# The first image of a two-layer state-space kernel: its convolution split over four engines, and the next image's norm placed ahead of it

## Chip, cores and metric

The kernel runs on one core of one Trainium2 chip (trn2). The metric is the device time of one execution in microseconds (us); less is better. Engines are named as in the profile: PE (TensorE; PEld its weight loads), DVE (VectorE), ACT (ScalarE), POOL (GpSimd), SP (SyncE, which here only issues DMAs).

## What is computed

Eight images of 64 x 64 positions and 96 channels go through two layers. Each layer normalizes the image in groups (32 groups of 3 channels, over the whole image), projects it to 192 channels and a gate z of 192, runs a depthwise 3 x 3 convolution with Silu over the 192, scans the result in four directions with a state of 16 per channel, sums the four, normalizes over channels, multiplies by Silu(z), projects back to 96 and adds the input. Cut to what matters here (layer 0):

```python
def _gn(v, G=32, eps=1e-5):
    g = v.reshape(B_, H_, W_, G, C_ // G)
    m = jnp.mean(g, axis=(1, 2, 4), keepdims=True)
    s = jnp.var(g, axis=(1, 2, 4), keepdims=True)
    return ((g - m) / jnp.sqrt(s + eps)).reshape(v.shape)
...
xz = x @ in_proj_w.T
xp, z = (xz[..., :Di], xz[..., Di:])
xc = conv_general_dilated(xc, conv_w, (1, 1), 'SAME', feature_group_count=Di) + conv_b
xc = _silu(xc)
...
dA = jnp.exp(d_t[..., None] * A)
h = dA * h + d_t[..., None] * B_e * u_t[..., None]
...
x = x + _L0_conv_ref(_gn(x), ...)
```

## The kernel before

Channels lie on partitions: 192 channels are two halves of C = 96 (NH = 2), positions run along the free axis. An image has L = 4096 positions, in four tiles of T = 1024 or eight of MM = 512[...].

The program is `begin`, then for each image the scan (`scan_rows`), and between two images `between`, which finishes one layer and makes the first deltas of the next image; `finish` ends the last image. The convolutions of later images are made piece by piece beside the scan (`conv_beside`, L1001), so only two convolutions stand alone: that of image 0 in `begin` (`conv_first`, L333) and that of layer 1 of the last image in `finish` (`conv_second`, L359). Both call one helper, `convolution` (L235).

What `convolution` does depends on `pe_rows` and `tap_rows`. The first half of the channels is convolved by PE in rows 0 to `pe_rows`: `by_pe` (L261) makes nine matmuls per 8 rows straight from the normalized image xn, with projection and tap folded into one weight (L264; in fp32 each matmul is two passes in the trace), and ACT takes the sum through Silu (L273). Rows beyond `pe_rows` of that half are projected into xp0 (`project`, L250; matmul L252, ACT copy L259); then ACT multiplies them by each tap (`first`, L293; L298) and POOL adds the terms (L300), and one Silu ends them (L331). The terms have two buffers. The second half of the channels is projected into xp1, and DVE applies the nine taps in PSUM (`second`, L278; first tap L287, the others L289), `tap_rows` rows at once, ACT taking each block out with Silu (L291). In the kernel before, `conv_first` passes `pe_rows` = HH = 64, so that nothing is left for ACT and POOL, and `tap_rows` = 8, and all of it shares two PSUM banks; `conv_second` passes PE_ROWS = 40 and `tap_rows` = 16, with four banks for products and one buffer of two banks for taps.

`conv_first` loads image 0 in eight pieces (L341, x_in, two buffers), DVE takes statistics of each (L160), POOL copies it into xn (L344), `group_norm` makes mean and root (PE L175, tiny ACT operations L185), DVE normalizes xn (L348), and the convolution follows. After it, `first_deltas` (L1605) makes what the scan needs to start: projections to x_dbl (PE L568, ACT L579), and for two jobs the deltas (PE L610, ACT L622 to L637, DVE L657 to L659, POOL L663), which are stored to DRAM (L673). Then `first_norm` (L1595) makes the norm of image 1: eight loads x_st (L1601), statistics and `group_norm`. Its result is first used when image 1's convolution runs beside image 0's scan.

In the scan a group is 32 channels times 4 states on 128 partitions; four sets of 4 states make a group, six groups a tile of 1024 positions, and 4 tiles in 4 directions an image: 96 groups. For each group replicas of 512 KB are loaded: dt_rep and dtu_rep (L526); for the first group of a tile also b_rep and c_rep of all four sets (L536). For each set ACT makes the decay (L869, in PSUM), DVE (L903) or, for the last set of a group, POOL (L893) the driving product from dtu_rep and b_rep, DVE the recurrence (L916), POOL the product with c_rep (L932), and PE gathers (L968). `low_rows` (L552; load L557) fetches the rows of x_dbl from which PE (L610) makes the arguments of the next deltas, which ACT takes at L622.

Engines and SP's queue issue in order. From the scans on, the order of instructions is written out by hand (`manual_schedule`); `begin` and the convolution in `finish` are outside of it, so that a scheduler orders them by readiness. The trace shows the two kinds mingled where they meet: SP issues L1601 between loads of L526 and L536. Pools (`tile_pool`) are areas of memory: what is opened after another has closed lies in the same place.

Of the kernel before, what the change touches and what calls it, by code (L numbers as in the profile page):

```python
# [8 lines left out]
F32 = mybir.dt.float32  # L9
AF = mybir.ActivationFunctionType  # L10
ALU = mybir.AluOpType
PSUM = bass.MemoryType.PSUM
# [3 lines left out]
NB, HH, WW, C = 8, 64, 64, 96  # L16
L = HH * WW
NH = 2
D = NH * C
N, R, K = 16, 6, 4  # L20
T = 1024
NT = L // T
MM = 512
SUB = T // MM
P = 128
# [6 lines left out]
PE_ROWS = 40  # L32
# [18 lines left out]
def two_ss2d_layers(ctx: ExitStack, tc: tile.TileContext, t: dict, out: bass.AP):  # L51
# [16 lines left out]
    keep = ctx.enter_context(tc.tile_pool(name="keep", bufs=2))  # L68
# [80 lines left out]
    def late_conv(l, pool):  # L149

        load_late(pool, f"in{l}", f"cw{l}", f"cb{l}")

        tap = pool.tile([C, 9, C], F32, name=f"tap{l}")
        nc.sync.dma_start(tap, t[f"cwt{l}"][0].unsqueeze(0).broadcast_to([C, 9, C]))
        own = w[f"in{l}"][:, :C].unsqueeze(1).broadcast_to([C, 9, C])
        nc.vector.tensor_tensor(tap, tap, own, ALU.mult)
        w[f"tap{l}"] = tap

    def chunk_stats(st, i, chunk):
        nc.vector.bn_stats(st[:, i, :], chunk)  # L160

    def stats_tile():
        return small.tile([C, L // MM, nc.vector.BN_STATS_DIM], F32, name="bn_st")
# [50 lines left out]
    def group_norm(st, bank):  # L214

        stages, got = group_norm_stages(st, bank)
        nc.scalar.preload_act_table_set("natural_log_exp_and_others")
        for stage in stages:
            stage()
        return got["gm"], got["r"], got["shift"]  # L220

    def grid(ap):
        return ap.rearrange("p (a b) -> p a b", b=WW)

    def padded(pool, name, first=True, rows=HH + 2):

        xp = pool.tile([C, rows, WW + 2], F32, name=name)
        nc.gpsimd.memset(xp[:, :, 0:1], 0.0)
        nc.gpsimd.memset(xp[:, :, WW + 1 : WW + 2], 0.0)
        nc.gpsimd.memset(xp[:, rows - 1, :], 0.0)  # L230
        if first:
            nc.gpsimd.memset(xp[:, 0, :], 0.0)
        return xp
# [96 lines left out]
        if left:  # L330
            nc.scalar.activation(rest, rest, AF.Silu)  # L331

    def conv_first(src, xc, pool, bank):  # L333

        rows = T // WW
        late_conv(0, pool)
        xn = padded(pool, "xn0")
        st = stats_tile()
        for i in range(L // MM):
            piece = pool.tile([C, MM], F32, name="x_in0", bufs=2)  # L340
            nc.sync.dma_start(piece, src[:, i * MM : (i + 1) * MM])  # L341
            chunk_stats(st, i, piece)
            r = 1 + i * MM // WW
            nc.gpsimd.tensor_copy(xn[:, r : r + MM // WW, 1 : 1 + WW], grid(piece))  # L344
        gm, gr, shift = group_norm(st, bank)
        for i in range(NT):
            at = xn[:, 1 + i * rows : 1 + (i + 1) * rows, 1 : 1 + WW]
            nc.vector.tensor_scalar(at, at, gm, gr, ALU.subtract, ALU.mult)  # L348
        convolution(0, xn, xc, pool, bank, bank, HH, MM // WW)
        return gm, gr, shift  # L350

    def stage_second(x1T, xn, i, norm):
# [37 lines left out]
    def scan_parts(b):  # L390

        units, jobs, sets = [], [], []
        for k in range(K):
            order = range(NT) if k < 2 else range(NT - 1, -1, -1)
            for nth, i in enumerate(order):
                unit = dict(k=k, nth=nth, t0=i * T, column=k % 2 == 1, backward=k >= 2)  # L400
                unit.update(short=False, n=T)
                units.append(unit)
                for h in range(NH):
                    jobs.append(dict(unit=unit, h=h))
                    for g in range(NG):
                        group = dict(unit=unit, job=jobs[-1], h=h, g=g)
                        sets += [
                            dict(unit=unit, group=group, i=i, first=h == g == i == 0)
                            for i in range(NS)
                        ]  # L410
        if b >= 1:
            unit, more_jobs, more = short_parts(b - 1)
            units, jobs, sets = units + [unit], jobs + more_jobs, sets + more
        x_dbl = [dram.tile([2 * ROWS, L], F32, name=f"x_dbl{c}", bufs=2) for c in "rc"]
        return units, jobs, sets, x_dbl
# [680 lines left out]
    def windows(first, n, b):  # L1096

        found = []
        last = K * NT * NH - (0 if b >= 1 else NH)
        for m in range(first, first + n):  # L1100
            at = m * PER - 1
            unit = m // NH + 2
            projects = m % NH == 1 and (unit < K // 2 * NT or b >= 1 and unit == K * NT)
            assert m < last
            if b >= 1 and m + NH >= K * NT * NH:
                found.append((at + 10, (3, 3, 3), 1))
            elif projects:
                found.append((at + 5, (3, 3, 3), 1))
            else:
                found.append((at + 3, (3, 2, 2, 2), 2))  # L1110
        return found

    def next_map(b, i):

        if i == 0:
            maps[b] = keep.tile([C, NH, L], F32, name="map")
        at = slice(i * T, (i + 1) * T)
        nc.sync.dma_start(maps[b][:, :, at], xc_far[b][:, :, at])

    def beside(b, pool):  # L1120


        def make(pmisc):
            plan = {}

            edged = pool.tile([C + 1, MM // WW + 2, WW + 2], F32, name="edged")
            nc.gpsimd.memset(edged[:C], 0.0)
            nc.gpsimd.memset(edged[C:], 1.0)
            if b >= 1:
                xc1_far[b - 1] = dram.tile([C, NH, L], F32, name="xc1_far", bufs=2)  # L1130
                xs[b - 1] = pool.tile([C, NH, HT], F32, name="x_short")
                conv_beside(
                    plan, pmisc, pool, edged, 1, x1[b - 1], xc1_far[b - 1], norm1[b - 1],
                    windows(0, 16, b), xs[b - 1],
                )
            if b + 1 < NB:
                xc_far[b + 1] = dram.tile([C, NH, L], F32, name="xc_far", bufs=2)
                conv_beside(
                    plan, pmisc, pool, edged, 0, t["x"][b + 1], xc_far[b + 1], norm0[b + 1],
                    windows(16 if b >= 1 else 0, 16, b),  # L1140
                )
                for i, step in enumerate((376, 378, 380, 388)):
                    plan.setdefault(step, []).append(lambda i=i: next_map(b + 1, i))
            return plan

        return make
# [448 lines left out]
    def first_norm(b, bank):  # L1595

        st = stats_tile()
        with tc.tile_pool(name="stats", bufs=2) as pool:
            for i in range(L // MM):
                piece = pool.tile([C, MM], F32, name="x_st")  # L1600
                nc.sync.dma_start(piece, t["x"][b][:, i * MM : (i + 1) * MM])  # L1601
                chunk_stats(st, i, piece)
        return group_norm(st, bank)

    def first_deltas(b, xc, pool, bank):  # L1605

        units, jobs, sets, x_dbl = parts = scan_parts(b)
        stages = projection(xc, x_dbl, units[0], pool, bank)
        for job in jobs[:NH]:
            stages += ready(xc, x_dbl, job, pool, bank, by_pe=False)  # L1610
        stages += projection(xc, x_dbl, units[1], pool, bank)
        return parts, [stage for _, stage in stages]

    def begin():

        with tc.tile_pool(name="pfirst", bufs=2, space=PSUM) as pfirst:
            bank = lambda name: pfirst.tile([P, MM], F32, tag="mm", name=name)
            xc = keep.tile([C, NH, L], F32, name="map")
            with tc.tile_pool(name="first", bufs=1) as pool:
                norm0[0] = conv_first(t["x"][0], xc, pool, bank)  # L1620
            with tc.tile_pool(name="before", bufs=1) as pool:
                parts, stages = first_deltas(0, xc, pool, pfirst)
                for stage in stages:
                    stage()
            if NB > 1:
                norm0[1] = first_norm(1, bank)
        return xc, parts

    def finish_first(b, y, st, xpool):
# [197 lines left out]
    x1 = dram.tile([NB, C, L], F32, name="x1")  # L1827
    xc_far, xc1_far, ys_far, xs, maps, norm0, norm1 = ({} for _ in range(7))
    xc, parts = begin()

    with tc.manual_schedule():
        for b in range(NB):
# [6 lines left out]
            if b + 1 < NB:  # L1839
                xc, parts = between(b, y)  # L1840
# [101 lines left out]
```

## Time and profile before

| What | us |
|---|---|
| three runs | 12340.3, 12369.4, 12373.6 |
| median | 12369.42 |
| the profiled execution | 12341.47 |
| its span in the profile | 12339.6 |
| first scan (L916) starts | 200.78 |
| last image's own convolution, DVE's first to ACT's last | 12097.5 to 12160.8 |

A time without a date is a duration; times such as 200.78 count from the span's start. A row of a timeline has a start, a duration over all instructions merged in it, engine (SPq: SP's issuing of a DMA), line, operation, output <- input with partitions x elements and type, how many, and in brackets the idle time before and what ended it. A wait is put down to the one that came last.

### The profile page before, as it was taken

The numbers are of one execution on the slowest core, as the hardware profiler recorded it, in microseconds if no ns is written. First come the engines' busy times: TensorE is split into PE (matmuls) and PEld (weight loads), VectorE is DVE, ScalarE is ACT, GpSimd is POOL, SyncE is SP. The second block draws the span as 40 slices with busy tenths as digits, with TensorE's granted clock in tenths as the row PEclk, the third lists the DMA queues.
The fourth block names the chain that finished last, engine by engine and source line by source line (L and its number), as shares of the span: only waits on it lengthen the run. The fifth ranks groups of instructions, "written<-read, shape, count | busy, mean of one in ns | idle before, by whom it ended". The sixth has DMA issues, their size and how long they took to land. (4 is left out here: it accounts for less than half of the span.)

```text
span 12339.6 us, 134054 instructions
## 1 busy us (share of the span) xinstructions
PE 9488.0 (77%) x44276; PEld 3013.1 (24%) x44276; DVE 10889.7 (88%) x6819; ACT 9677.8 (78%) x15172; POOL 10439.8 (85%) x4748
## 2 busy tenths in 40 slices
PE   5875578887887778887788777888778887887567
PEld 1221122222222222222222222222222222222122
DVE  6999889997999969999699997999879998799985
ACT  4888778887787867888778787887878887788875
POOL 3999889996899969999699996999869998799973
PEclk8877778888888878888788888887888887888778
DMA  3444444444444444444444444444544445444441
GB/s 96 166 148 155 134 159 159 154 159 144 158 162 161 163 133 166 152 157 163 137 163 161 161 152 150 152 158 160 159 137 165 160 155 163 132 161 159 157 144 58
DMA packets 670623, 1861.52 MB, mean 151 GB/s; under 512 B 186824, under 2 KB 201454, under 8 KB 669917
## 3 DMA queue, kind: packets, MB, share of 16 engines
q1 hardware_dynamic: 662749, 1840.28, 45.1%
q10 hardware_dynamic: 7168, 12.59, 0.3%
q8 instruction: 351, 5.75, 0.2%
q14 instruction: 355, 2.91, 0.1%
HBM read 1539.31 MB, written 313.28 MB: 150 GB/s over the span
## 5 line engine op out<-in xcount | busy, mean ns | idle before, releaser
L932 POOL TENSOR_TENSOR out<-set,c_rep 128x1024 f32<-128x1024 f32 x3120 | 7295.1, 2358 | 905.9 <-DVE set L916 315.7
L916 DVE TENSOR_TENSOR_SCAN set<-decay,state,set 128x1024 f32<-128x1024 f32 x2304 | 5365.7, 2345 | 390.4 <-ACT decay L869 176.2
L869 ACT ACTIVATE decay<-dt_rep,w_a 128x1024 f32<-128x1024 f32 x3072 | 3420.2, 1114 | 332.9 <-DVE set L916 327.3
L903 DVE TENSOR_TENSOR set<-drive,b_rep 128x1024 f32<-128x1024 f32 x2352 | 2817.1, 1198 | 47.6 <-DMA b_rep<-x_dblr 39.1
L1035 PE MATMUL ps_conv<-edged,taps 96*96 96x512 f32 (+1 forms) x4032 | 2435.7, 743 | 54.7 <-ACT z L623 26.3
L968 PE MATMUL acc<-out,w_gather 128*32 128x256 f32 x24576 | 2271.9, 479 | 9.7 <-POOL out L932 9.6
L916 DVE TENSOR_TENSOR_SCAN set<-decay,set 128x1024 f32<-128x1024 f32 x768 | 1744.4, 2286 | 226.6 <-ACT decay L869 148.0
L893 POOL TENSOR_TENSOR set<-dtu_rep,b_rep 128x1024 f32<-128x1024 f32 x768 | 1811.2, 2358 | 97.0 <-DMA b_rep<-x_dblr 58.4
L959 PE MATMUL acc<-map,w_eye 96*32 96x256 f32 x4608 | 565.5, 572 | 1513.4 <-ACT map L998 1277.0
L998 ACT COPY map<-acc 32x256 f32<-32x256 f32 x3072 | 1472.7, 479 | 45.9 <-PE acc L968 5.6
L968 PEld LDWEIGHTS acc<-out,w_gather 128*32 128x32 f32 x24576 | 782.5, 130 | 1925.3 <-issue 1279.6
L1035 PEld LDWEIGHTS ps_conv<-edged,taps 96*96 96x96 f32 (+1 forms) x4032 | 718.8, 197 | 1383.1 <-issue 1220.3
L927 ACT COPY state<-set 128x1 f32<-128x1 f32 x2304 | 426.0, 185 | 761.4 <-DVE set L916 754.5
L642 PE MATMUL ps_sp<-z,w_eye 96*96 96x512 f32 x960 | 657.2, 773 | 287.9 <-ACT ln L651 244.6
L663 POOL TENSOR_TENSOR dtu<-ln,map 96x1024 f32<-96x1024 f32 x256 | 670.4, 2619 | 243.4 <-DVE ln L659 133.8
L886 ACT COPY drive<-dtu_rep 128x1024 f32<-128x1024 f32 (+1 forms) x816 | 813.6, 997 | 36.3 <-DMA dtu_rep<-dtu_far 31.0
L610 PE MATMUL ps_dt<-x_dbl,w_dtw 7*96 7x512 f32 x1024 | 594.7, 662 | 302.9 <-ACT z L623 150.9
L959 PEld LDWEIGHTS acc<-map,w_eye 96*32 96x32 f32 x4608 | 100.7, 120 | 1978.5 <-ACT map L998 1673.4
L642 PE MATMUL ps_sp<-dtu,w_eye 96*96 96x512 f32 x960 | 553.4, 661 | 0.0
L642 PE MATMUL ps_sp<-ln,w_eye 96*96 96x512 f32 x960 | 535.5, 642 | 0.0
L622 ACT ACTIVATE dt<-ps_dt 96x512 f32<-96x512 f32 x512 | 303.3, 592 | 279.7 <-PE ps_dt L610 261.0
L642 PE MATMUL ps_sp<-dt,w_eye 96*96 96x512 f32 x960 | 507.1, 611 | 0.0
(202 smaller groups left out, 9328.6 us busy)
## 6 DMA issues: line engine op xcount, KB each, us to landing
dt_rep<-dt_far SPq DMA_DIRECT2D x768, 512.0 KB
dtu_rep<-dtu_far SPq DMA_DIRECT2D x768, 512.0 KB
b_rep<-x_dblr SPq DMA_DIRECT2D x256, 512.0 KB
c_rep<-x_dblr SPq DMA_DIRECT2D x256, 512.0 KB
b_rep<-x_dblc SPq DMA_DIRECT2D x256, 512.0 KB
c_rep<-x_dblc SPq DMA_DIRECT2D x256, 512.0 KB
dt_far<-ln SPq DMA_DIRECT2D x256, 384.0 KB
dtu_far<-dtu SPq DMA_DIRECT2D x256, 384.0 KB
```

Source lines behind the costliest of these rows:

```text
L642: nc.tensor.matmul(job["ps"][:C, :], w["eye"], job[term][:, halves[s]], start=i == 0, stop=i == 3,)
L663: nc.gpsimd.tensor_tensor(like(job["dtu"], col), like(job["dt"], col), positions(xc[:, h, :], col, t0, T), ALU.mult,)
L869: nc.scalar.activation(s["decay"], s["group"]["dt"], AF.Exp, scale=rate)
L886: nc.scalar.copy(s["group"]["drive"], s["group"]["dtu"])
L893: nc.gpsimd.tensor_tensor(s["buf"], s["group"]["dtu"], b, ALU.mult)
L903: nc.vector.tensor_tensor(s["buf"], s["group"]["drive"], b, ALU.mult)
L916: nc.vector.tensor_tensor_scan(ordered(s["buf"], unit), ordered(s["decay"], unit), ordered(s["buf"], unit), 0.0 if unit["nth"] == 0 else s ...
L932: nc.gpsimd.tensor_tensor(s["out"], s["buf"], s["unit"]["c", s["i"]], ALU.mult)
L959: nc.tensor.matmul(acc, lhs[:, GC * g : GC * (g + 1)], positions(old[:, h, :], unit["column"], unit["t0"] + at, n), start=True, stop=False ...
L968: nc.tensor.matmul(acc, w["gather"], s["out"][:, at : at + n], start=False, stop=s["i"] == NS - 1, skip_group_check=True,)
L998: nc.scalar.copy(yk, like(acc, unit["column"]))
L1035: nc.tensor.matmul(job["ps"][:C, :], taps[l][:k, h, tap, :], edged[:k, tap // 3 : tap // 3 + rows, tap % 3 : tap % 3 + WW], start=tap == 0 ...
```

## The change

`conv_first` now calls the convolution with PE_ROWS and 16-row taps, as `conv_second` does, and gets banks in the same manner: a pool of four banks and one buffer of two for taps. Ahead of the convolution it calls `beside()`, which is `first_norm(1, ...)`: image 1's norm, no longer behind the first deltas. The deltas get PSUM from a pool of their own, opened after those of the convolution have closed.

```diff
-    def conv_first(src, xc, pool, bank):
+    def conv_first(src, xc, pool, bank, tap_bank, beside):
...
             nc.vector.tensor_scalar(at, at, gm, gr, ALU.subtract, ALU.mult)
-        convolution(0, xn, xc, pool, bank, bank, HH, MM // WW)
+        beside()
+        convolution(0, xn, xc, pool, bank, tap_bank, PE_ROWS, T // WW)
         return gm, gr, shift
...
     def begin():
 
-        with tc.tile_pool(name="pfirst", bufs=2, space=PSUM) as pfirst:
-            bank = lambda name: pfirst.tile([P, MM], F32, tag="mm", name=name)
-            xc = keep.tile([C, NH, L], F32, name="map")
-            with tc.tile_pool(name="first", bufs=1) as pool:
-                norm0[0] = conv_first(t["x"][0], xc, pool, bank)
-            with tc.tile_pool(name="before", bufs=1) as pool:
-                parts, stages = first_deltas(0, xc, pool, pfirst)
-                for stage in stages:
-                    stage()
-            if NB > 1:
-                norm0[1] = first_norm(1, bank)
+        xc = keep.tile([C, NH, L], F32, name="map")
+        with (
+            tc.tile_pool(name="first", bufs=1) as pool,
+            tc.tile_pool(name="pmm", bufs=4, space=PSUM) as pmm,
+            tc.tile_pool(name="ptap", bufs=1, space=PSUM) as ptap,
+        ):
+            bank = lambda name: pmm.tile([P, MM], F32, tag="mm", name=name)
+            tap_bank = lambda name: ptap.tile([P, T], F32, name=name)
+
+            def second_image():
+                if NB > 1:
+                    norm0[1] = first_norm(1, bank)
+
+            norm0[0] = conv_first(t["x"][0], xc, pool, bank, tap_bank, second_image)
+        with (
+            tc.tile_pool(name="before", bufs=1) as pool,
+            tc.tile_pool(name="pfirst", bufs=2, space=PSUM) as pfirst,
+        ):
+            parts, stages = first_deltas(0, xc, pool, pfirst)
+            for stage in stages:
+                stage()
         return xc, parts
```

## The prediction

> **What bounds it now.** The busy shares of the page (DVE 88%, POOL 85%, PE 77%) are means over eight images; this change lies in the first 200 us, before the first scan, so I read that stretch alone, first by windows.
>
> Windows of the kernel before; columns: stretch, length, then busy us (instructions) of PE, PEld, DVE, ACT, POOL, then granted PE clock, DMA share, GB/s.
> ```profile
> 0.00:46.00 46.00, 0.95 (x4) 0.78 (x4) 16.66 (x29) 4.85 (x16) 9.83 (x29) 1.00 0.32 88
> 46.00:137.00 91.00, 76.34 (x162) 27.27 (x163) 55.46 (x76) 15.28 (x25) 0.00 (x0) 1.00 0.00 0
> 137.00:171.00 34.00, 14.07 (x24) 3.72 (x22) 8.46 (x7) 21.33 (x26) 4.68 (x2) 0.65 0.40 130
> 171.00:200.00 29.00, 2.88 (x6) 1.18 (x6) 5.59 (x9) 2.90 (x8) 1.44 (x3) 0.50 0.68 205
> ```
> The convolution of image 0 (46 to 137) is PE's: POOL idle, ACT 15 us busy. 137 to 171 are the first deltas, a chain over PE, ACT, DVE, POOL. In 171 to 200 every compute engine stands and only DMA works. Who they stand for, in the list of waits from 135 to 260 (columns: who, line, for whom: us, times, longest):
> ```profile
> ACT gn_less L185 <- PE ps_pm L175: 31.1, 1, 31.1
> POOL out L932 <- issue: 27.4, 1, 27.4
> DVE bn_st L160 <- DMA x_st<-in_x: 21.8, 4, 13.2
> ```
> ACT waits for the second image's norm; its decays (L869) come behind, and the first scan starts at 200.78, the fifth at 213.49 (DVE's timeline).
>
> **The stage has two twins in the same trace.** The last image's convolution (12094 to 12161) already runs with PE_ROWS = 40 and 1024-element taps. Timelines there; columns: start, us, engine, line, operation, idle before and releaser.
> ```profile
> 12097.50 1.34 DVE L287 TENSOR_SCALAR ps_tap<-xp,w_cw,w_cb 96x1024 f32<-96x1024 f32 x1 [0.68 <-POOL xp L230]
> 12118.74 1.34 DVE L287 TENSOR_SCALAR ps_tap<-xp,w_cw,w_cb 96x1024 f32<-96x1024 f32 x1 [9.26 <-ACT map L291]
> 12134.81 1.34 DVE L287 TENSOR_SCALAR ps_tap<-xp,w_cw,w_cb 96x1024 f32<-96x1024 f32 x1 [4.10 <-ACT map L291]
> 12104.28 28.08 POOL L300 TENSOR_TENSOR map<-map,term 96x1536 f32<-96x1536 f32 x8 [6.79 <-ACT term L298]
> 12159.82 1.02 ACT L291 ACTIVATE map<-ps_tap 96x1024 f32<-96x1024 f32 x1 [11.40 <-DVE ps_tap L289]
> ```
> Four DVE blocks of 12.0 us, with stalls of 9.26, 4.10 and 1.09: the single ps_tap buffer is emptied by ACT (L291), which stands in order behind terms (L298) that wait for POOL's adds. From POOL's first add to the end: 12160.84 - 12104.28 = 56.6 us. The second twin is image 1's scan start, with no norm before it:
> ```profile
> 1566.28 0.57 SPq L526 DMA_DIRECT2D dt_rep<-dt_far  x1
> 1576.15 0.28 SPq L557 DMA_DIRECT2D x_dbl<-x_dblr  x1
> 1590.77 0.59 ACT L622 ACTIVATE dt<-ps_dt 96x512 f32<-96x512 f32 x1 [15.28 <-PE ps_dt L610]
> 1592.97 2.29 DVE L916 TENSOR_TENSOR_SCAN set<-decay,set 128x1024 f32<-128x1024 f32 x1 [10.99 <-ACT decay L869]
> ```
> Two scans run, then ACT stands 15 us at L622: PE's L610 needs x_dbl, a small load queued behind ten 512 KB replicas. The fifth scan starts at 1599.73, 9.0 after L622. So without the norm the start is bound by DMA's fill.
>
> **What the Trainium skill says.** "TensorE: Matmul & The Clock Gate", section "What's actually happening": PE runs at half clock after an idle window (about 3.4 us) and at full clock after about that long busy. The trace agrees in kind: half-passes of L252 and L264 start 0.85 us apart at 46 to 51 and again after 62.2, and 0.43 from 68.6 on; here that took 5.4 to 6.6 us. "GPSIMD Engine Reference", section "3.1 Elementwise — side-by-side cycle accounting": about 2.6 cycles per element for two inputs, so some 3.3 us (estimate, at 1.2 GHz) for 1536; the trace has 28.08 / 8 = 3.51. "DMA: Bandwidth & Descriptors", section "Issuing engines are not separate DMA queues": all issues share the same 16 engines; so loads moved away make room for those left. The fill here moves 200 to 350, in the mean 260 GB/s.
>
> **The change, part by part.**
>
> *Convolution.* Removed: three of eight PE blocks (54 half-passes) and 72 DVE taps of 512 elements (0.78 us apart with the first of each block). Added: nine ACT terms (1.58 each), eight POOL adds (28.1 together), one ACT Silu of 1536 (1.48), four small projections into xp0, its memsets, and 36 DVE taps of 1024 (48 us). Four PSUM banks plus two of its own for taps replace two shared. PE needs 5 x 8.6 = 43 us and is no longer last. In the twin PE was warm; here projections begin cold at 46.06: three of them at 1.7, to 51.5, then the fourth plus two warm, to about 55; two terms on ACT (3.2), so POOL's first add at about 59.1. End 59.1 + 56.6 = 115.7, without what the norm adds.
>
> *The norm in front.* Moved: eight x_st loads of 192 KB on SP, eight statistics (0.68) and an aggregate (0.37) on DVE, two tiny products (four passes, 1.0) on PE, twelve tiny ACT operations (3.2) and the table preload. SP passes it ahead of everything of the deltas and the scan; DVE, PE and ACT ahead of the convolution. x_st has two buffers of its own, so its loads lie beside those of x_in (88 GB/s in 0 to 46, against 260 that DMA can do); DVE idles 2.2 of every 3.4 us there, so 5.5 us of statistics fit. ACT idles 2.7 us until the first projection and 1.1 between copies. Were this cover gone, the loads would be serial: 14 us, and 5 of norm chain. Bounds 0 (all hidden; a gain has no source) and 19; I take 3: some 2 for sharing DMA, 1 on ACT. Convolution's end: 118.7.
>
> *The deltas* open their pools when the convolution's close. I take it that they wait for the whole pool: x_st at 174.26 waited for dtu's store, the last of pool "before", though its own place had long been free. Before, the first projection (L568) began at 136.57, warm; now PE has idled since about 102, and eight half-passes plus two (L610) run at 0.86 instead of 0.44: L622 comes 8.0 after the start instead of 4.65, so 3.3 lost. Deltas gain 136.6 - 118.9 - 3.3 = **14.4 us**; bounds 2 (norm unhidden) and 27 (DVE's stalls gone).
>
> *Norm removed from the scan's start.* On the old clock: dt_rep issues at 156.79, but image 0's second delta stores (168.38, 170.94) stand in SP's queue, so the replicas c1, b2, c2, dt, dtu, b3, c3 go out from 171.3. By 170 DMA has moved 3.7 MB (windows of 3 us summed), which is all issued but the last stores; left are 0.79 + 7 x 0.524 = 4.45 MB, at 260 GB/s 17.1 us. c3, and x_dbl behind it, land at about 187.3 instead of 197.5. Then as in image 1: L622 0.6 later, the fifth scan 9.0 after that, 197. Before 213.49: **16 us** gained, not the 33 that the stall from 167.8 (when b_rep, the drive and a table load allow a first decay) to 200.8 suggests. What is late next is x_dbl. Bounds 12 (240 GB/s and two more us) and 23.5, if ACT reached its decays and only b3 (landing at about 184, then POOL's L893 at 2.35) held the fifth scan. Scan, norms and plan of all later images are the same instructions in the same order, so the shift carries to the end.
>
> Sum 14.4 + 16 = 30.4, say 31 us: 12341.5 - 31 = 12310 against the profiled execution (span 12339.6, 1.9 around it). The three runs gave 12340.3, 12369.4 and 12373.6; the profiled one stands with the lowest, 28 below the median. Against the median: **12338 us**, -0.25%. 0.3%, 37 us, is about what a measurement of this kernel can tell from no change.
>
> **Rivals.**
>
> *More: the order on ACT is kinder than in the twin.* There memsets of xp (L230) held DVE's first tap until 12097.5; in the first image they ran early (23.75), so DVE may finish block 1 sooner against ACT's terms, and its L291 may stand ahead of some. Without the 9.26 and 4.10 the convolution ends 13 us earlier: 44 us, 12325. Against it: the same helper is ordered by the same scheduler. Chance 0.30.
>
> *Less: the norm in front isn't covered.* ACT and DVE are in order; if a statistic or gn_less stands ahead of L259 or L287 and its x_st is late, the convolution stands too. Between my 3 and 19: 15, so a gain of 19, 12350. For it: the 21.8 us of waits for x_st now, beside big replicas; against: no replicas at 25 to 40. Chance 0.18.
>
> *Slower: the first scan runs out of step.* The hole after scan two leaves POOL behind DVE; POOL has 5 x 2.35 = 11.75 us of work in a group of 13.2. If it doesn't catch up, each of image 0's 96 groups (4 directions x 4 tiles x 6) loses a little: from 31 / 96 = 0.32 us per group the change costs time, at 0.7 it is 67 - 31 = 36 us slower, 12406. For it: image 1, which starts so, gets 376 scans into 1287 us where image 0 gets 380; against: it carries work for the image before besides, and after 1599.7 its groups take 13.3. Chance 0.06.
>
> *It does nothing to the start:* the scheduler leaves the norm's ACT chain late. Its pools close ahead of the deltas, so only the convolution's own time could suffer; chance 0.02, inside "less". My forecast has 0.46.
>
> **Numbers.** Faster by over 0.3% needs 37 us: most of "more" (0.25), and the upper part of my case with the runs' scatter of 30 us (0.21): 0.46. Slower by over 0.3%: 0.06. Within: 0.48. Range 12302 to 12360: from "more" less 23 for the runs' scatter to "less" with 10 of it; it leaves out the slow case and the far end of a fast one.
>
> **What would show it.** Right: four blocks of L289 at 1285 ns with two longer stalls for L291; POOL's L300 eight times from about 62; convolution over near 119; L568 cold; no x_st behind 60; first scan near 153, two scans, then ACT at L622 for over 10 us; fifth scan near 213.5 - 30 = 183. Wrong: deltas starting before the last L291; a wait of L259 or L287 for the norm; a fifth scan before 172 or after 200; group times in the first image that differ from 13.2.

## The result, and the profile after

Eight runs of each kernel, taken together: before 12349.63 us median, after 12310.47, ratio **0.9963 [0.9951, 0.9975]**, so 39 us (0.37%) less. The profiled execution of after took 12308.22, its span 12306.4, which is 33.2 below the span before. Lines from L349 on have numbers higher by one in after: L568 is L569, L610 L611, L622 L623, L869 L870, L893 L894, L916 L917. Of the experiments below, e1, e6 and e7 happen to have a line fewer and so the numbers of before there.

The windows of after; columns as before.
```profile
46.00:60.00 14.00, 12.10 (x26) 4.87 (x27) 10.04 (x10) 9.61 (x24) 0.00 (x0) 1.00 0.00 1
60.00:104.00 44.00, 39.29 (x91) 14.39 (x89) 28.16 (x23) 21.77 (x22) 27.55 (x8) 1.00 0.00 1
104.00:136.00 32.00, 16.09 (x19) 4.69 (x20) 14.94 (x12) 14.39 (x19) 2.34 (x1) 0.55 0.07 22
136.00:170.00 34.00, 7.20 (x10) 1.59 (x8) 12.15 (x9) 13.73 (x17) 9.57 (x7) 0.55 0.76 237
```
Between 60 and 104 POOL and ACT now carry 28 and 22 us of the convolution, and PE is through at about 100 instead of 136. In the last stretch DMA is busy 76% of the time (237 GB/s), with every compute engine mostly idle: the scan's start waits for loads.

Timelines of after, by engine; columns: start, us, engine, line, operation, idle before and releaser.
```profile
47.51 2.98 DVE L348 TENSOR_SCALAR xn<-xn,gn_gm,gn_r 96x1024 f32<-96x1024 f32 x4 [3.63 <-ACT gn_r L185]
...
74.48 1.34 DVE L287 TENSOR_SCALAR ps_tap<-xp,w_cw,w_cb 96x1024 f32<-96x1024 f32 x1 [9.74 <-ACT map L291]
...
90.58 1.34 DVE L287 TENSOR_SCALAR ps_tap<-xp,w_cw,w_cb 96x1024 f32<-96x1024 f32 x1 [4.12 <-ACT map L291]
...
146.84 2.28 DVE L917 TENSOR_TENSOR_SCAN set<-decay,set 128x1024 f32<-128x1024 f32 x1
...
169.50 2.29 DVE L917 TENSOR_TENSOR_SCAN set<-decay,set 128x1024 f32<-128x1024 f32 x1 [7.52 <-ACT decay L870]
...
176.26 2.29 DVE L917 TENSOR_TENSOR_SCAN set<-decay,set 128x1024 f32<-128x1024 f32 x1
...
60.03 28.10 POOL L300 TENSOR_TENSOR map<-map,term 96x1536 f32<-96x1536 f32 x8 [17.56 <-ACT term L298]
...
115.59 1.02 ACT L291 ACTIVATE map<-ps_tap 96x1024 f32<-96x1024 f32 x1 [11.41 <-DVE ps_tap L289]
...
119.31 0.59 ACT L623 ACTIVATE dt<-ps_dt 96x512 f32<-96x512 f32 x1 [1.55 <-PE ps_dt L611]
...
167.29 0.59 ACT L623 ACTIVATE dt<-ps_dt 96x512 f32<-96x512 f32 x1 [20.00 <-PE ps_dt L611]
...
104.24 6.90 PE L569 MATMUL ps_proj<-map,w_wx 96*78 96x512 f32 x8 [4.03 <-ACT map L273]
```
Read down the engines. The DVE stalls of the twin (9.26, 4.10) are here as 9.74 and 4.12. POOL's adds run from 60.03, and ACT's last L291 ends the convolution at 116.61, 56.6 after the first add, as in the twin. The first scan starts at 146.84 instead of 200.78; two scans run, ACT stands 20.0 us at L623 with the decays of the next scans behind it, and the fifth scan starts at 176.26 instead of 213.49: **37.2 us earlier**. The last row is the one that the prediction ruled out: PE starts the deltas' first projection at 104.24, twelve us before the convolution ends, released by L273.

Who the start waits for, in the list of waits from 135 to 260 (who, line, for whom: us, times, longest):
```profile
PE ps_dt L611 <- DMA x_dbl<-x_dblr: 25.6, 1, 25.6
ACT dt L623 <- PE ps_dt L611: 20.9, 4, 20.0
POOL set L894 <- DMA b_rep<-x_dblr: 9.8, 1, 9.8
```
The norm's L185 and the loads x_st are gone from it. x_dbl is the new holder.

The gain does not stay exactly 37. By the issue of the first dt_rep of images 1 to 7 after stands ahead of before by 42.3, 43.3, 46.9, 40.7, 25.8, 33.3 and 29.9 us, and at the last image's own convolution (12064.49 against 12097.50) by 33.0. The scans between are the same instructions; from one image to the next the lead shrinks by up to 15 us and grows by up to 7.5. Why is not shown.

### The profile page after: what moved, and what is told of

Read it like the earlier page. It is cut to its first block, busy times and chain, and to the rows that moved or that the text cites. A ratio compares the mean times of both kernels' runs of the same rounds, so it can differ in the third digit from the quotient of the medians.

```text
span 12306.4 us, 133952 instructions
## 1 busy us (share of the span) xinstructions
PE 9479.3 (77%) x44230; PEld 3010.0 (24%) x44230; DVE 10887.0 (88%) x6783; ACT 9692.5 (79%) x15179; POOL 10466.1 (85%) x4759
## 5 line engine op out<-in xcount | busy, mean ns | idle before, releaser
L917 DVE TENSOR_TENSOR_SCAN set<-decay,state,set 128x1024 f32<-128x1024 f32 x2304 | 5365.3, 2345 | 412.0 <-ACT decay L870 202.9
L870 ACT ACTIVATE decay<-dt_rep,w_a 128x1024 f32<-128x1024 f32 x3072 | 3420.4, 1114 | 337.9 <-DVE set L917 331.0
L1036 PE MATMUL ps_conv<-edged,taps 96*96 96x512 f32 (+1 forms) x4032 | 2464.4, 751 | 53.8 <-ACT z L624 27.1
L917 DVE TENSOR_TENSOR_SCAN set<-decay,set 128x1024 f32<-128x1024 f32 x768 | 1744.1, 2286 | 229.5 <-ACT decay L870 154.0
L894 POOL TENSOR_TENSOR set<-dtu_rep,b_rep 128x1024 f32<-128x1024 f32 x768 | 1809.1, 2356 | 107.0 <-DMA b_rep<-x_dblr 53.6
L611 PE MATMUL ps_dt<-x_dbl,w_dtw 7*96 7x512 f32 x1024 | 593.7, 661 | 340.0 <-ACT z L624 148.2
L887 ACT COPY drive<-dtu_rep 128x1024 f32<-128x1024 f32 (+1 forms) x816 | 813.7, 997 | 36.4 <-DMA dtu_rep<-dtu_far 30.9
L623 ACT ACTIVATE dt<-ps_dt 96x512 f32<-96x512 f32 x512 | 303.0, 592 | 306.7 <-PE ps_dt L611 287.4
```

What stands on the lines that cost most here:

```text
L870: nc.scalar.activation(s["decay"], s["group"]["dt"], AF.Exp, scale=rate)
L887: nc.scalar.copy(s["group"]["drive"], s["group"]["dtu"])
L894: nc.gpsimd.tensor_tensor(s["buf"], s["group"]["dtu"], b, ALU.mult)
L917: nc.vector.tensor_tensor_scan(ordered(s["buf"], unit), ordered(s["decay"], unit), ordered(s["buf"], unit), 0.0 if unit["nth"] == 0 else s ...
L1036: nc.tensor.matmul(job["ps"][:C, :], taps[l][:k, h, tap, :], edged[:k, tap // 3 : tap // 3 + rows, tap % 3 : tap % 3 + WW], start=tap == 0 ...
```

## The experiments

**1 and 2. Each half of the change alone.** The theory: two gains that add. The rivals: an earlier convolution only lengthens the norm's stall (e1); or all 33 us of the stall are the norm's, and nothing takes their place (e2).

```diff
 # e1, from after: the split alone; the norm behind the deltas again, in PSUM of its own
-        beside()
         convolution(0, xn, xc, pool, bank, tap_bank, PE_ROWS, T // WW)
...
             for stage in stages:
                 stage()
+        with tc.tile_pool(name="pnorm", bufs=2, space=PSUM) as pnorm:
+            bank = lambda name: pnorm.tile([P, MM], F32, tag="mm", name=name)
+            norm0[1] = first_norm(1, bank)
```


> The convolution's split alone; image 1's norm stays between the deltas and the scan, in a PSUM pool of its own. Theory (the two parts add up): the convolution ends at 116.6 - 2.3 = 114.3, as no norm lies in front (xn's normalization again at 45.2 instead of 47.5); the first dt_rep issues 23 us before that of the kernel before (156.8), near 134, and the norm then costs the same stall as before, so that the fifth scan starts near 190.5 instead of 213.5: 23 us gained, ratio to before about 0.9981. Rival (the norm's stall is set by DMA and ends at a time that an earlier convolution doesn't move): fifth scan still beyond 205, gain under 9 us.

```diff
 # e2, from before: the norm in front alone; PE still makes 64 rows, taps still of 8 rows
+        beside()
         convolution(0, xn, xc, pool, bank, bank, HH, MM // WW)
...
-            if NB > 1:
-                norm0[1] = first_norm(1, bank)
```


> The norm's place alone; the convolution as before (all of its first half on PE, 512-element taps, two shared banks). Theory: normalization of xn at 47.5, convolution 2.3 us late, dt_rep near 159, then the same fill as in the changed kernel (dt_rep to fifth scan 40.1 us, ACT standing some 20 us at the first argument of the third job for x_dbl): fifth scan near 199, 14 us gained, ratio about 0.9988. Together with the split alone 37, what the changed kernel gains. Rival (all 33 us of the stall are the norm's): fifth scan near 182, 31 us gained, ratio 0.9975.

The split alone gives a ratio of 0.9985 [0.9971, 0.9999], the norm alone 0.9987 [0.9978, 0.9995]. In the profiles the fifth scan starts at 192.17 and 198.79, 21.3 and 14.7 us before the 213.49: sum 36.0, together 37.2. Timelines, first ACT and DVE of e1, then ACT of e2:
```profile
175.12 0.17 ACT L185 ACTIVATE gn_less<-ps_pm 96x1 f32<-96x1 f32 x1 [33.46 <-PE ps_pm L175]
...
179.47 2.29 DVE L916 TENSOR_TENSOR_SCAN set<-decay,set 128x1024 f32<-128x1024 f32 x1 [4.97 <-ACT decay L869]
```
```profile
189.83 0.59 ACT L623 ACTIVATE dt<-ps_dt 96x512 f32<-96x512 f32 x1 [19.75 <-PE ps_dt L611]
```
With the norm left in its place ACT stands 33.5 us for it, much as before (31.1); with only the norm moved, ACT stands 19.75 for L611. Neither rival holds (they wanted the fifth scan beyond 205 in e1 and near 182 in e2). So the two halves add at the fifth scan; the totals agree, but their intervals are too wide to tell a sum from its parts. What replaces the norm's wait is L611, which reads x_dbl. In after its releaser is x_dbl itself; in e2 the profile names a c_rep, which SP issues just ahead of it. That x_dbl is the holder rests on experiment 5. The front norm's price shows as well: xn is normalized from 47.51 in after and 47.58 in e2, from 45.19 in before and 45.97 in e1, so the price is 1.5 to 2.4 us.

**3. Is the early projection due to which PSUM banks it gets?** A bank is what the code calls one PSUM tile of 128 x 512 fp32. The theory: the deltas' pool lies where `pmm` lay, the first pool opened, so each of its banks is free when L273 has read it; nothing waits for the whole convolution. The rival: the scheduler merely found PE idle, and the place does not matter. Only the order of two pools is changed, so that the deltas get the banks of the taps.
```diff
-            tc.tile_pool(name="pmm", bufs=4, space=PSUM) as pmm,
             tc.tile_pool(name="ptap", bufs=1, space=PSUM) as ptap,
+            tc.tile_pool(name="pmm", bufs=4, space=PSUM) as pmm,
```


> The changed kernel with the two PSUM pools of the convolution opened in the other order, so that the deltas' two banks lie where the taps' buffer was and not where the products' were; every engine's order of instructions is the same. Theory (a PSUM bank is waited for by itself, and the deltas' first projection could start 12 us ahead of the convolution's end because its banks had been let go by the last product): L569 now starts after the last L291, near 116.7 instead of 104.2, cold, L623 near 124 instead of 119.3, everything behind some 4.5 us later, fifth scan near 181. Rival (the projection waited for nothing but its data and PE's order): no change, L569 at 104, fifth scan at 176.

Timelines of PE and ACT:
```profile
117.09 6.03 PE L569 MATMUL ps_proj<-map,w_wx 96*78 96x512 f32 x8 [16.42 <-ACT map L291]
...
124.18 0.59 ACT L623 ACTIVATE dt<-ps_dt 96x512 f32<-96x512 f32 x1 [0.34 <-PE ps_dt L611]
```
The releaser is now L291, the last instruction of the convolution (its end: 117.04), and the projection starts with it. L623 comes 7.1 us after the end, where after has 2.7; the fifth scan starts at 182.24, 6.0 later than in after: 4.1 at dt_rep's issue, the rest in the fill behind it. The theory holds so far: the place decides, and nothing waits for the whole convolution. Whether the wait goes by the bank or by the pool that held it is not told apart: by the order in which the code hands out the four banks, the last L273 is the last reader both of the deltas' first bank and of `pmm`. This was one execution (12298.85); its total, inside the runs of after, says nothing on six us.

**4. A second tap buffer.** The theory: the stalls of 9.74 and 4.12 come from the single ps_tap; with two the convolution ends some 13 us earlier (the "more" rival's amount). The rival: ACT and POOL bound the convolution themselves, and its end moves by under 4 us.
```diff
-            tc.tile_pool(name="ptap", bufs=1, space=PSUM) as ptap,
+            tc.tile_pool(name="ptap", bufs=2, space=PSUM) as ptap,
```


> The changed kernel with two buffers for the taps' PSUM tile in the first convolution. Theory (DVE's stalls of 9.7, 4.1 and 1.1 us are the single buffer, which ACT empties late since it stands behind terms that wait for POOL): DVE's four blocks run from 52.8 with under 3 us of stalls, the convolution ends near 103.6 instead of 116.6, the fifth scan starts near 163, 13 us earlier; ratio to the kernel before about 0.9959 by the traces. Rival (ACT and POOL bound the convolution themselves: POOL's adds end at 88 and ACT's Silus follow): the end moves by under 4 us.

The convolution ends at 112.69, only 3.9 earlier (51.9 after POOL's first add instead of 56.6), and the ratio, 0.996 [0.9947, 0.9973], is that of after. A miss for the theory, and just within the rival's mark. DVE's, ACT's and PE's timelines:
```profile
84.56 1.34 DVE L287 TENSOR_SCALAR ps_tap<-xp,w_cw,w_cb 96x1024 f32<-96x1024 f32 x1 [6.53 <-ACT xp L259]
...
81.91 1.58 ACT L298 ACTIVATE term<-xp,w_cw 96x1536 f32<-96x1536 f32 x1 [1.94 <-POOL map L300]
83.39 0.67 ACT L273 ACTIVATE map<-ps_cv,w_cb 96x512 f32<-96x512 f32 x1
83.96 0.57 ACT L259 COPY xp<-ps_in 96x512 f32<-96x512 f32 x1
...
101.43 3.66 PE L569 MATMUL ps_proj<-map,w_wx 96*78 96x512 f32 x8 [0.77 <-ACT map L273]
```
DVE no longer waits for L291 but for L259, the copy of its next rows; and that copy stands in ACT's order behind a term (L298) that waits for POOL. That suggests a third reading: neither the buffer nor POOL's amount of work, but ACT's order. Experiment 6 tries it.

**5. x_dbl's rows issued earlier.** The theory: the start is held by the small load x_dbl behind the replicas. It is moved ahead of the last four replicas in the order written out by hand; this touches every image's start, not only the first.
```diff
-                plan.setdefault(-1, []).insert(0, lambda: low_rows(x_dbl, units[1], rows))
+                plan.setdefault(-2, []).insert(0, lambda: low_rows(x_dbl, units[1], rows))
```


> The changed kernel, with low_rows (the small load x_dbl) one step earlier in every image's scan: ahead of the last four of the ten first replicas instead of behind all. Theory (what holds the scan's start once the norm is gone is this load, at the end of DMA's fill; ACT stands at the arguments of the third job, and the decays behind it): ACT no longer stands there; the third scan follows b_rep at once, the fourth waits for POOL's product of the last b_rep, and the fifth starts near 172.5 in image 0 instead of 176.3 and some 7 us earlier in each of the seven later images (1551 instead of 1558 in image 1, less 4): some 50 us together, ratio to the kernel before about 0.992. Rival (the replicas themselves hold the start): b_rep's wait takes the place of the other, the fifth scan moves by under 2 us, ratio 0.996.

Timelines of ACT and DVE:
```profile
164.20 0.59 ACT L623 ACTIVATE dt<-ps_dt 96x512 f32<-96x512 f32 x1 [14.02 <-PE ps_dt L611]
...
169.55 0.87 ACT L1029 ACTIVATE edged<-edged,gn_shift,gn_r 96x576 f32<-96x576 f32 x1 [3.17 <-DMA edged<-in_x]
...
171.36 1.12 ACT L870 ACTIVATE decay<-dt_rep,w_a 128x1024 f32<-128x1024 f32 x1
...
172.57 2.29 DVE L917 TENSOR_TENSOR_SCAN set<-decay,set 128x1024 f32<-128x1024 f32 x1 [3.87 <-ACT decay L870]
```
ACT's wait falls from 20.0 to 14.0: the first L611 starts 23.7 after dt_rep's issue instead of 29.1, the third scan 27.9 instead of 33.3 and the fifth 37.6 instead of 40.1. (By the clock the fifth starts at 176.08, no earlier than in after, since the convolution of this execution ended 2.3 later.) At the starts of images 1 to 7 the fourth scan comes 27.4 after dt_rep in the mean, in after 31.2, in the other six kernels that leave the load in its place 30.2 to 30.8. So x_dbl did hold it, but the gain is at most some two thirds of what was expected: 2.5 of 3.7 in image 0, 4.5 of 7 at image 1's fifth scan (29.4 after dt_rep, in after 33.9). The timeline of SP has twelve replicas ahead of the load where the expectation has ten: dt_rep and dtu_rep of two groups, b_rep and c_rep of four sets. So it still lies behind eight, and in image 0 the next in line shows: the fourth scan's decay (171.36) stands on ACT behind L1029, which waits 3.17 us for the load of edged, a piece of image 1 for its convolution. The ratio is 0.9947 [0.993, 0.9965], median 12302.27. Seven starts at some 3 to 3.8 make 21 to 27 us, of which the profiled execution (12309.58, near the upper end of its runs) shows nothing in its total; e5 against after is not settled by these runs.

**6. All projections first, four term buffers.** If ACT's order is what holds DVE (experiment 4), all copies L259 ahead of the terms, and terms that need not wait for POOL, should free it. This is e4 with two edits in the helper.
```diff
-            out = pool.tile([C, left * WW], F32, name="term", bufs=2) if tap else rest
+            out = pool.tile([C, left * WW], F32, name="term", bufs=4) if tap else rest
...
-        for r in range(0, 3 * step, step):
+        for r in range(0, HH, step):
...
-            project(1, r, step, xp1, 1 + r)
```


> Two tap buffers as in e4, and besides all projections of xp1 ahead of the terms and four term buffers instead of two (in the shared helper, so in the last image's convolution too). Theory (in the changed kernel ACT's order is what DVE waits for: behind terms held up by POOL stand both the Silus that empty the taps' buffer and the copies that fill xp1; with a second buffer alone the second kind took the place of the first): DVE's four blocks run with under 3 us of stalls, the convolution ends near 103 instead of 116.6 and 112.7 (e4). Rival (POOL's adds and the Silu behind them are the bound): it ends beyond 109.

Timelines of DVE, ACT and PE:
```profile
78.08 1.34 DVE L287 TENSOR_SCALAR ps_tap<-xp,w_cw,w_cb 96x1024 f32<-96x1024 f32 x1 [3.19 <-ACT map L291]
...
100.48 1.02 ACT L291 ACTIVATE map<-ps_tap 96x1024 f32<-96x1024 f32 x1 [2.81 <-DVE ps_tap L289]
101.40 0.67 ACT L273 ACTIVATE map<-ps_cv,w_cb 96x512 f32<-96x512 f32 x1
...
102.13 6.98 PE L568 MATMUL ps_proj<-map,w_wx 96*78 96x512 f32 x8 [2.41 <-ACT map L273]
```
One stall of 3.2 is left, and the convolution, whose last instruction is now L273, ends at 102.07, 14.5 earlier: so the rival does not hold, and DVE was held by what stood ahead of its copies and Silus on ACT, not by the amount of work. Which of the two edits in the helper, the order or the buffers for terms, did how much was not tried apart. Only 9.8 of it reach the fifth scan (166.48), because the projection's cover goes: it starts after the convolution's end, its eight half-passes at 0.87, and ACT's L622 comes 8.1 after the end instead of 2.7. This too was one execution (12299.33).

**7. All three, in both convolutions.** e5 and e6, and two tap buffers in `conv_second` as well.
```diff
 # conv_second, and the line of experiment 5
-            tc.tile_pool(name="ptap", bufs=1, space=PSUM) as ptap,
+            tc.tile_pool(name="ptap", bufs=2, space=PSUM) as ptap,
```


> e5 and e6 together, with two tap buffers in the last image's convolution too. If both theories hold: 13 us in the first convolution, 13 in the last, some 50 at the scans' starts, on top of the change: 12340 - 39 - 76, near 12235, ratio to the kernel before about 0.991. If e5's rival holds: 0.994.

Ratio to before **0.9913 [0.9899, 0.9927]**, median 12252.87 against 12350.8, as expected (0.991): this version beats both kernels, since the interval of after's ratio begins at 0.9951. The profile shows the fifth scan at 164.72 (48.8 before the kernel before), the fourth scan of images 1 to 7 again 27.4 after dt_rep in the mean, and the last image's own convolution with one long stall:
```profile
12032.46 1.34 DVE L287 TENSOR_SCALAR ps_tap<-xp,w_cw,w_cb 96x1024 f32<-96x1024 f32 x1 [5.66 <-ACT map L291]
...
12054.41 1.02 ACT L291 ACTIVATE map<-ps_tap 96x1024 f32<-96x1024 f32 x1 [0.92 <-DVE ps_tap L289]
```
From its first tap (12004.77) to its end 50.7 us, where before took 63.3.

## Why the prediction was right, and where it was not

**Right: the front norm.** Predicted 3 us, of bounds 0 to 19; xn came 2.3 later (47.51 against 45.19; 1.5 against e1), and the rival "less" fell with it: no L259 or L287 waits for the norm.

**Right: the convolution.** Predicted end 118.7 = 62.1 + 56.6. POOL's first add came at 60.03, two us sooner, and the 56.6 held to the tenth, in e1, e3 and e5 too. The two us are PE's cold start, which differs from one execution to the next: e5, with the same instructions up to here, has its first add at 62.33. The twin in `finish` was a good measure: helper, buffers and ACT's stalls were the same.

**Failed: "I take it that they wait for the whole pool".** Predicted: the deltas start with the convolution's end, cold, and L622 comes 8.0 after it. Measured: L569 starts 12.4 us before the end and L623 comes 2.7 after it. Only PE's part came early: ACT takes the first product (L580) at 116.51, right behind its last L291. The evidence used, an x_st that waited for the last store of a closed pool, was a load into SBUF, and no run shows what it lay on; experiment 3 shows that the deltas' wait in PSUM is for what last read the place that they get, and not for the end of all the convolution's pools. The cold clock itself was as the Trainium skill has it ("TensorE: Matmul & The Clock Gate", section "What's actually happening"): half-passes of L569 at 6.90 / 8 = 0.86 us in after, 3.60 / 8 = 0.45 in before. In after PE had stood 4.03 us just before, in e4 only 0.77, and there the same eight take 3.66. But in after the cold projection lay beside DVE's last block and cost nothing: e4, warm, has its L623 2.7 after the convolution's end too. Uncovered, a cold start cost about what was predicted, 3.3: L622 came 8.0 after the projection's start in e6 and 7.1 in e3, where PE warmed up on the way, against the warm 4.65. The term in the sum: deltas 14.4 predicted, measured 20.6 at dt_rep (156.79 to 136.21). The 6.2 are 2.3 for the earlier end (116.6, where the sum has the deltas start at 118.9) and 5.3 for L623's 2.7 instead of 8.0, less some 1.3 that the rest of the deltas took longer; 0.7 of that is lost by the second L623, whose L611 runs cold.

**Right: the scan's start.** Predicted 16, not the 33 of the visible stall, because x_dbl behind the fill takes the norm's place. Measured 37.2 - 20.6 = 16.6, with ACT 20.0 us at L623. e2, where it is alone, agrees: 14.7 with the front norm's price in it, 16.2 counted from dt_rep's issue. "What is late next" was the decisive question here. The ten replicas ahead of x_dbl are a slip: the timelines have twelve, and so does the sum (five out before 171.3, then seven), so that its 17 us stand. Every transfer of this stretch is issued by SP, so that nothing here tests what the prediction cites of issues from several engines.

**The sum.** 31 predicted, 37.2 at the fifth scan, 33.2 in the span, 39 in the medians. That the span comes so near the 31 is luck: 6 us more at the fifth scan, and then the lead, as high as 46.9 and as low as 25.8 between images, happens to end at 33. The 39 lie just over the 37 that the prediction set as the border of a clear gain; it gave the side beyond it 0.46 and its own side, within, 0.48. The predicted absolute, 12338, lies 28 above the median of after; that is the difference between the median of the three runs shown (12369) and the profiled execution, on which the sum of 12310 was made. With eight runs before's median is 12349.6: the three were a high draw, and the profiled execution was nearer to what is typical.

**The rivals.** "More" has nearly the size (44 against 37) and not the mechanism: the stalls of 9 and 4 us that it wanted gone are there. "Slower" needed 0.32 us lost in each of image 0's 96 groups; from the fifth scan to image 1's dt_rep after takes 1524.03 - 176.26 = 1347.8 us, before 1566.28 - 213.49 = 1352.8, so none is lost.

## What to carry to other kernels

When a visible stall is removed, price what is late next, not the stall: here 33 us of standing were worth 16. A twin of the stage elsewhere in the same trace can give a duration, stalls included, that is hard to get from a sum of parts (56.6 here), but only inside the stage; how the stage joins the next has to be asked buffer by buffer: who last reads the place that the next instruction writes. And where one engine empties another's buffer in program order, look at that order before adding a buffer: here the buffer alone took 3.9 us off and moved the stall to ACT's next duty, and with the order changed as well it was 14.5.

## What was not expected of the hardware

- **A small load is as late as the fill it stands in.** From dt_rep's issue to the first L611 there passed 29.1 us in after, and 29.6, 30.9, 32.1 and 29.2 in e2, e3, e4 and e6 with the same twelve replicas; in e5, with four of them behind it, 23.7. So between these executions the fill varies by 3 us, which hides or feigns small gains ahead of it: that is how e4's 3.9 became 0.9 at the fifth scan. Whether the kernel or chance makes the 3 us is not shown.
- **PE's cold start is not of one length.** At the head of the convolution the first sixteen half-passes (L252) take 8.60 us in after and 11.01 in e5, with the same instructions and the same start (48.4 and 48.3): single profiles of two kernels can differ by 2 us here for no reason that lies in their instructions.
- **The scatter of a kernel's runs goes with the mean clock granted to PE.** e2's 22 runs go from 12386.0 at 0.803 to 12305.9 at 0.812; over all kernels with several runs it is about 4.9 us for 0.001, with correlations of -0.59 to -0.97 inside each. The mean clocks of the compared sets differ (before 0.8065 and e7 0.8102 in their comparison, e5 0.8055), so some 18 of e7's 98 us may belong to it. For the comparison of before and after, 39 us, the clocks of before's runs are not recorded (after's mean is 0.8066). Whether the clock is cause or sign was not tried.
